# Attention scores by half pieces: column scores and row scores in the two halves of the same PSUM banks

## The chip, the cores and the metric

The kernel runs on one core of one Trainium2 chip. The metric is the device time of one execution in microseconds. The kernel before took 2210.52 us (median of three runs, 2204.25 to 2211.26).

## What is computed

The reference is a two-layer perceiver. 32 batches of 64 latent rows with 256 features go through a first layer (a linear mix with the mean of a context, self-attention, a routed mixture of experts) and a second layer (cross-attention to the context, a convolution with a gated recurrence, a feed-forward block with quantised weights). The part that this change touches is the cross-attention of the second layer, whose context has 1601 rows a batch:

```python
q = _split_heads(query @ Wq.T + bq)      # 16 heads of 16
k = _split_heads(bank @ Wk.T + bk)
v = _split_heads(bank @ Wv.T + bv)
scores = jnp.einsum('bhqd,bhkd->bhqk', q / score_scale, k)
attn = jax.nn.softmax(scores, axis=-1)
ctx = jnp.einsum('bhqk,bhkd->bhqd', attn, v)
return ctx.transpose(0, 2, 1, 3).reshape(b, sq, MODEL_DIM) @ Wo.T + bo
```

All of it is done in float32, but for a bf16 carrier of the maxima that is described below.

## The kernel before, in words

The 2048 latent rows are 16 tiles (`NT`) of 128 rows, each of two batches. For one tile the cross-attention is cut into four halves (two batches by two groups of eight heads), and the context of a half into three pieces of 512 rows (`PIECE`), with a tail of 65 rows (`TAIL`) that all four halves share as one more piece. So a tile has 13 pieces (`NU`), and the program has 208, numbered g.

A piece goes through these steps, each a function of g:

- `keys` (line 671): the projection of 512 context rows to keys, four matmul records of 512 columns on PE (each float32 matmul shows as two records), and one ACT step that adds the bias and leaves `kt` in SBUF (line 692).
- `row_scores` (line 713): the scores with latent rows on the partitions, 128 x 512 for each of four pairs of heads. The four pairs lie on the four row groups of PE's array (32 rows each) and write four banks, which are two tiles `ps[0]` and `ps[1]` of two banks. They serve only for the maximum along the context: two DVE reductions of 1024 elements (line 732; line 729 for the tail).
- `maxima` and `maxima_rows` (lines 734 and 745): when the three pieces of a half and the tail have been scanned, the negated maximum is split into three bf16 parts and transposed to `neg`.
- `column_scores` (line 752): the same scores with context rows on the partitions. A bf16 matmul (line 767, line 764 for the tail) first writes the negated maxima, then 16 float32 matmuls of 128 columns (line 773) add the scores. Again two tiles of two banks; two ACT exponentials of 1024 elements (line 779) write `pt`.
- `values` (line 694): the projection of the piece to values, 16 records on PE, and a DVE copy to one of five buffers `vau` (line 709).
- `weighted` (line 782): 64 records of 64 columns (line 797) add the weighted values of a piece, and a row of ones beside them the denominators, to one accumulator `w.o` in PSUM (pool `ps_o`, one buffer), which is copied to `w.osb` at the tile's end (lines 802 and 804).
- `normalise` (line 806): one quarter of a tile is divided by its sums, with a matmul, a reciprocal (line 815) and a product (line 816).

The score tiles of both kinds come from one pool `ps_sc` with two buffers (line 63), so the four banks are used in turn by columns and rows. Everything else that goes through PSUM shares three banks (`mm_tile`).

The order on PE, DVE, ACT and POOL is that of the program, written out by hand. The loop at line 1256 does for each g: the columns of g, the values of g+4, a share of the other layers' work (`run(g, 0)`), the rows of g+5, the weighted values of g, the keys of g+6, and another share (`run(g, 1)`). The other layers' work (first layer of later tiles, second layer of earlier tiles, routing) consists of generators whose steps `run` deals out by a table of first and last times (lines 1194 to 1209); steps whose result ACT has to take go to place 0 in some of them, the others to place 1. Ahead of the loop the rows of the pieces 0 to 4 are scanned without columns (line 1234). Loads run on SP's queue: `load_batch` (line 1005) brings the context of a batch, 1601 KB, and is called for the next tile at the pieces 2 and 9 of a tile.

Of the kernel before, what the change touches and what calls it, by code (L numbers as in the profile page):

```python
# [9 lines left out]
F32 = mybir.dt.float32  # L10
# [15 lines left out]
NF = 6  # L26
HID = 1024
PIECE = 512
NP = L // PIECE
TAIL = L - NP * PIECE  # L30
NU = 4 * NP + 1
# [13 lines left out]
def perceiver_kernel(ctx: ExitStack, tc: tile.TileContext, a: dict, out: bass.AP):  # L45
# [17 lines left out]
    def sc_tile(name):  # L63
        return ps_sc.tile([P, 2, 512], F32, tag="sc", name=name)
# [571 lines left out]
    def split(g):  # L636

        pos, p = divmod(g, NU)
        if p == 3 * NP:
            return pos, None, None  # L640
        p -= p > 3 * NP
        return pos, 4 * pos + p // NP, p % NP

    def scanned(g):

        pos, p = divmod(g, NU)
        return (pos, 4 * pos + (p - 1) // NP, (p - 1) % NP) if p else (pos, None, None)
# [62 lines left out]
            v[:kr, :, 0:VW - 16].rearrange("p k (h d) -> p k h d", d=17)[:, :, :, 0:16],  # L710
            o[:kr].rearrange("p k (h d) -> p k h d", d=16))

    def row_scores(g):


        pos, h, k = scanned(g)
        w, qbd = wholes[pos], queries[pos]
        if h is None:
            w.mx = small.tile([P, 4, 4, NP + 1], F32, tag="mx1", name=f"mx1_{w.ti}", bufs=2)
        ps = [sc_tile(f"r_{g}_{m}") for m in range(2)]  # L720
        for q in range(4) if h is None else [h % 4]:
            for i in range(4):
                r = slice(32 * i, 32 * i + 32)
                o = ps[i // 2][:, i % 2, :] if h is not None else ps[i // 2][:, i % 2, q * TAIL:(q + 1) * TAIL]
                nc.tensor.matmul(o, lhsT=qbd[r, q % 2, q // 2].rearrange("p h q -> p (h q)"),  # L725
                                 rhs=w.kt[r, q, :] if h is None else halves[h].kt[k][r, :], start=True, stop=True)
        for m in range(2):
            if h is None:
                nc.vector.tensor_reduce(w.mx[:, 2 * m:2 * m + 2, :, NP],
                                        ps[m][:, :, :4 * TAIL].rearrange("p i (q l) -> p i q l", q=4), AX.X, ALU.max)  # L730
            else:
                nc.vector.tensor_reduce(w.mx[:, 2 * m:2 * m + 2, h % 4, k], ps[m], AX.X, ALU.max)  # L732

    def maxima(h):

# [13 lines left out]
        hf.neg = work.tile([P, P], BF16, tag="neg", name=f"neg_{hf.name}", bufs=5)  # L749
        nc.vector.tensor_copy(hf.neg, t)  # L750

    def column_scores(g):

        pos, h, k = split(g)
        w, qbd = wholes[pos], queries[pos]
        ps = [sc_tile(f"s_{g}_{m}") for m in range(2)]
        kr = TAIL if h is None else P
        for i in range(4):
            r = slice(32 * i, 32 * i + 3)
            o = ps[i // 2][:kr, i % 2, :]  # L760
            if h is None:

                for q in range(4):
                    nc.tensor.matmul(o[:, q * P:(q + 1) * P], lhsT=onesb[r, :kr], rhs=halves[4 * pos + q].neg[r, :],
                                     start=(q == 0), stop=False)
            else:
                nc.tensor.matmul(o, lhsT=onesb[r, :], rhs=halves[h].neg[r, :].unsqueeze(1).to_broadcast([3, 4, P]),  # L767
                                 start=True, stop=False)
        for j in range(4):
            q = j if h is None else h % 4  # L770
            for i in range(4):
                r = slice(32 * i, 32 * i + 32)
                nc.tensor.matmul(ps[i // 2][:kr, i % 2, j * P:(j + 1) * P],  # L773
                                 lhsT=w.kt[r, j, :] if h is None else halves[h].kt[k][r, j * P:(j + 1) * P],
                                 rhs=qbd[r, q % 2, q // 2].rearrange("p h q -> p (h q)"), start=False, stop=(j == 3))
        w.pt[g] = []
        for m in range(2):
            pt = big.tile([P, 2, 4, P], F32, tag="pt", name=f"pt_{g}_{m}", bufs=2)
            nc.scalar.activation(pt[:kr].rearrange("p i k c -> p i (k c)"), ps[m][:kr], AF.Exp)  # L779
            w.pt[g].append(pt)  # L780

    def weighted(g):

        pos, h, k = split(g)
        w = wholes[pos]
        first, last = g % NU == 0, g % NU == NU - 1
        if first:
            w.o = o_tile([P, 4, 2, S], f"o1_{w.ti}")
        v, pts = vau[g % 5], w.pt.pop(g)
        kr = TAIL if h is None else P  # L790
        for j in range(4):
            q = j if h is None else h % 4
            for m in range(2):
                for c in range(4):
                    hd = 4 * m + c

                    nc.tensor.matmul(w.o[32 * c:32 * c + 32, q, m, :], lhsT=v[:kr, j, 17 * hd:17 * hd + 32],  # L797
                                     rhs=pts[m][:kr, c // 2, j, c % 2 * S:c % 2 * S + S],
                                     start=(m == 0 and (first and j == 0 or h is None and j == 3)), stop=(m == 1 and (last and j == 3 or h is None and j == 2)))
        if h is None:  # L800
            w.osb = work.tile([P, 4, 2, S], F32, tag="osb", name=f"osb_{w.ti}", bufs=1)
            nc.vector.tensor_copy(w.osb[:, 0:3], w.o[:, 0:3])
        elif last:
            nc.vector.tensor_copy(w.osb[:, 3], w.o[:, 3])
# [407 lines left out]
    with tc.manual_schedule(engines={ET.PE, ET.DVE, ET.Activation, ET.Pool}):  # L1212
        ahead, beside, summing = Steps(first()), Steps(first_layer(1, 1)), Steps(early_sums())
        early = [lambda g=g: keys(g) for g in range(1, 4)] + [lambda: keys(0)] + [
            lambda g=g: values(g) for g in range(4)] + [lambda g=g: keys(g) for g in range(4, 6)]

        def others():
            if 0 in csums:
# [12 lines left out]
                late.pop()()  # L1231
        for f in early + late:
            f()
        for g in range(4):
            row_scores(g)
            others()
        maxima(0)
        row_scores(4)
        others()
        maxima_rows(0)  # L1240
        if beside.gen is not None:
# [14 lines left out]
        for g in range(NU * NT):  # L1256
            pos, p = divmod(g, NU)
            if pos + 1 < NT:
                if p == 0:
                    wholes[pos + 1].rest = load_rest(order[pos + 1])  # L1260
                if p in (2, 9):
                    load_batch(2 * pos + 2 + p // 8)
            column_scores(g)
            if g + 4 < NU * NT:
                values(g + 4)
            if p == 0 and pos:
                normalise(pos - 1, 3)
            elif p > 3 * NP:
                normalise(pos, p - 3 * NP - 1)
            if g + 4 < NU * NT and scanned(g + 4)[2] == NP - 1:  # L1270
                maxima_rows(scanned(g + 4)[1])
            run(g, 0)
            if g + 5 < NU * NT:
                row_scores(g + 5)
                if scanned(g + 5)[2] == NP - 1:
                    maxima(scanned(g + 5)[1])
            weighted(g)
            if g + 6 < NU * NT:
                keys(g + 6)
            if p == 1 and pos:  # L1280
                x4[pos - 1] = projected(pos - 1)
            run(g, 1)
        normalise(NT - 1, 3)
        x4[NT - 1] = projected(NT - 1)
        plan.append(Steps(second_layer(NT - 1)))
# [52 lines left out]
```

## Time and profile before

| | |
|---|---|
| median of three runs | 2210.52 us |
| the profiled execution's own time | 2210.8 us |
| its span | 2209.1 us |
| mean granted PE clock | 0.971 |
| DVE row maxima, 1024 elements (line 732) | 384 times, 1220 ns |
| ACT exponentials, 1024 elements (line 779) | 416 times, 1021 ns |
| PE row scores, records of 512 columns (line 725) | 1536, 228.5 us |
| PE column scores, records of 128 columns (line 773) | 6144, 209.4 us |
| PE bf16 maxima, records of 512 columns (line 767) | 768, 80.6 us |

The span is the time between the first and the last instruction of the profiled execution. In the page's rows, a group of instructions has its line, its engine, what it writes and reads, the busy time in us and the mean of one in ns, and after the second bar the idle time of the engine just before it and what ended it. PE is the matmul engine and PEld its weight loads, DVE the vector engine, ACT the scalar engine. Matmul records are pipelined: a record lasts longer than the distance to the next one, so distances between starts tell what a step costs.

### The profile page before, as it was taken

To read this page: it belongs to the slowest core of one execution; us is meant where nothing else is said; L and a number is where in the kernel's file an instruction comes from. 1 tells how busy PE (TensorE), PEld (TensorE's weight loads), DVE (VectorE), ACT (ScalarE), POOL (GpSimd) and SP (SyncE) were. 2 spreads that over 40 slices of the span, in tenths; PEclk is the share of its full clock that TensorE was granted. 3 is DMA by queue.
4 is the path that set the end of the run, shared out by engine and by line. 5 is a ranking of instruction groups with operands and counts; after the bars stand their busy time and mean duration, and the time that the engine had idled before them with its cause. 6 is when DMAs were issued, how large, how long until landed. Compare 5 with 4: busy or idle time off the path is not lost. (4 is left out here: it accounts for less than half of the span.)

```text
span 2209.1 us, 69768 instructions
## 1 busy us (share of the span) xinstructions
PE 2077.7 (94%) x31887; PEld 1520.5 (69%) x31903; DVE 1342.9 (61%) x2686; ACT 907.4 (41%) x1397; POOL 315.5 (14%) x525
## 2 busy tenths in 40 slices
PE   6799999999999999999999999999998899999984
PEld 4567677677676777777776776777776566677763
DVE  4556765666656566665665656565667656656554
ACT  3334444444435344444544444353433234334342
POOL 2111111111211111111111111111100000000011
PEclk8799999999999999999999999999999999999986
DMA  7223221111212111111211111101100101000000
GB/s 263 87 100 112 80 77 64 64 52 34 70 66 73 64 53 64 37 67 63 76 52 64 66 34 66 64 34 41 37 32 34 42 31 34 14 32 35 2 4 5
DMA packets 46175, 126.41 MB, mean 57 GB/s; under 512 B 12558, under 2 KB 28344, under 8 KB 45880
## 3 DMA queue, kind: packets, MB, share of 16 engines
q1 hardware_dynamic: 45320, 121.13, 16.0%
q8 instruction: 250, 4.10, 0.8%
q10 hardware_dynamic: 560, 0.81, 0.1%
q14 instruction: 45, 0.37, 0.1%
HBM read 119.83 MB, written 2.10 MB: 55 GB/s over the span
## 5 line engine op out<-in xcount | busy, mean ns | idle before, releaser
L779 ACT ACTIVATE pt<-s 128x1024 f32<-128x1024 f32 (+1 forms) x416 | 403.1, 1021 | 307.9 <-PE s L773 307.7
L732 DVE TENSOR_REDUCE mx<-r 128x2 f32<-128x1024 f32 x384 | 452.2, 1220 | 114.3 <-PE r L725 113.9
L233 PE MATMUL vps<-w_L_xattn_WvT,ctxT 128*128 128x128 f32 x3072 | 397.7, 283 | 0.0
L233 PE MATMUL kps<-ctxT,w_L_xattn_WkT 128*128 128x512 f32 x768 | 382.9, 622 | 11.4 <-DMA ctxT<-ctxT 11.4
L692 ACT ACTIVATE kt<-kps,chv 128x512 f32<-128x512 f32 x192 | 131.9, 687 | 636.7 <-PE kps L233 636.7
L709 DVE COPY vau<-vps 128x512 f32<-128x512 f32 (+1 forms) x208 | 143.3, 689 | 399.5 <-PE vps L233 399.5
L233 PEld LDWEIGHTS vps<-w_L_xattn_WvT,ctxT 128*128 128x128 f32 x3072 | 361.6, 193 | 24.1 <-issue 3.4
L797 PEld LDWEIGHTS o<-pt,vau 128*32 128x32 f32 (+1 forms) x13312 | 197.7, 111 | 150.9 <-issue 144.2
L797 PE MATMUL o<-pt,vau 128*32 128x64 f32 (+1 forms) x13312 | 232.3, 222 | 4.2 <-ACT pt L779 4.2
L725 PE MATMUL r<-kt,qbd 32*128 32x512 f32 x1536 | 228.5, 652 | 2.4 <-DVE mx L732 1.5
L233 PEld LDWEIGHTS kps<-ctxT,w_L_xattn_WkT 128*128 128x128 f32 x768 | 131.5, 191 | 123.0 <-issue 106.0
L773 PEld LDWEIGHTS s<-qbd,kt 32*128 32x128 f32 x6144 | 208.6, 189 | 3.2
L773 PE MATMUL s<-qbd,kt 32*128 32x128 f32 x6144 | 209.4, 273 | 0.0
L245 ACT ACTIVATE part<-part 128x1601 f32<-128x1601 f32 x60 | 92.6, 1543 | 16.2 <-DMA part<-ctxT 15.9
L725 PEld LDWEIGHTS r<-kt,qbd 32*128 32x128 f32 x1536 | 63.6, 186 | 40.8 <-issue 19.1
L767 PE MATMUL s<-neg,onesb 3*128 3x512 bf16 x768 | 80.6, 388 | 9.2 <-DVE mx L732 6.9
L767 PEld LDWEIGHTS <-onesb 3*128 3x128 bf16 x768 | 21.3, 91 | 97.6 <-issue 96.2
L815 DVE RECIPROCAL rs<-sums 128x128 f32<-128x128 f32 x64 | 60.7, 948 | 3.4 <-PE sums L812 3.3
L233 PE MATMUL ff<-nT,w_fg 128*128 128x128 f32 x384 | 51.7, 287 | 1.0 <-ACT nT L927 1.0
L311 POOL TENSOR_TENSOR kbd<-kT,mask 128x512 f32<-128x512 f32 x32 | 32.9, 1049 | 138.0 <-ACT kT L304 138.0
L233 PE MATMUL ff<-nT,w_fv 128*128 128x128 f32 x384 | 50.2, 283 | 0.0
L233 PEld LDWEIGHTS ff<-nT,w_fg 128*128 128x128 f32 x384 | 47.8, 201 | 1.9 <-ACT nT L927 1.8
(338 smaller groups left out, 2539.4 us busy)
## 6 DMA issues: line engine op xcount, KB each, us to landing
ctxT<-ctxT SPq DMA_DIRECT2D x32, 1601.0 KB, 6.9
part<-ctxT SPq DMA_DIRECT2D x60, 800.5 KB, 4.5
rest<-ctxT SPq DMA_DIRECT2D x32, 65.0 KB, 2.1
x<-x SPq DMA_DIRECT2D x16, 128.0 KB, 2.6
out<-x SPq DMA_DIRECT2D x16, 128.0 KB, 1.7
w<-w SPq DMA_DIRECT2D x16, 128.0 KB, 2.3
sum_L_ffn_w1T<-L_ffn_w1T SPq DMA_DIRECT2D x4, 256.0 KB, 6.7
raw_L_ffn_w1T<-L_ffn_w1T SPq DMA_DIRECT2D x4, 256.0 KB, 2.6
```

The source lines that it names most:

```text
L233: nc.tensor.matmul(o, lhsT=lhsT(c), rhs=rhs(c), start=(c == 0), stop=(c == 1))
L245: nc.scalar.activation(junk, src, AF.Copy, accum_out=csum[:, c, b:b + 1])
L311: nc.gpsimd.tensor_tensor(kbd[oc], kT[:, oc, :].rearrange("p (b k) -> p b k", b=2).unsqueeze(2).to_broadcast([P, 2, 4, S]), mask4.unsqueez ...
L692: nc.scalar.activation(kt, o, AF.Identity, bias=chv[:, hf.oc, BK2:BK2 + 1])
L709: nc.vector.tensor_copy(v[:kr, :, 0:VW - 16].rearrange("p k (h d) -> p k h d", d=17)[:, :, :, 0:16], o[:kr].rearrange("p k (h d) -> p k h ...
L725: nc.tensor.matmul(o, lhsT=qbd[r, q % 2, q // 2].rearrange("p h q -> p (h q)"), rhs=w.kt[r, q, :] if h is None else halves[h].kt[k][r, :], ...
L732: nc.vector.tensor_reduce(w.mx[:, 2 * m:2 * m + 2, h % 4, k], ps[m], AX.X, ALU.max)
L767: nc.tensor.matmul(o, lhsT=onesb[r, :], rhs=halves[h].neg[r, :].unsqueeze(1).to_broadcast([3, 4, P]), start=True, stop=False)
L773: nc.tensor.matmul(ps[i // 2][:kr, i % 2, j * P:(j + 1) * P], lhsT=w.kt[r, j, :] if h is None else halves[h].kt[k][r, j * P:(j + 1) * P], ...
L779: nc.scalar.activation(pt[:kr].rearrange("p i k c -> p i (k c)"), ps[m][:kr], AF.Exp)
L797: nc.tensor.matmul(w.o[32 * c:32 * c + 32, q, m, :], lhsT=v[:kr, j, 17 * hd:17 * hd + 32], rhs=pts[m][:kr, c // 2, j, c % 2 * S:c % 2 * S ...
L815: nc.vector.reciprocal(rs, t)
```

## The change

The scores are made by halves of a piece, 256 context rows at a time. For half 0 and again for half 1 of each piece, PE writes the column scores of piece g to the first 256 columns of each of the four banks, and right behind them the row scores of piece g+5 to the other 256 columns of the same banks. The exponentials and the maxima of a half then take 512 elements each, in the order exp 0, max 1, exp 1, max 0, so that ACT and DVE work on different tiles. The maxima of a half piece have a place of their own in `mx` (seven instead of four columns). `pt` has six buffers of half the size. The weighted values run half a piece behind: in the iteration of g PE adds the second half of g-1 and the first half of g. The values are made for g+3 instead of g+4, the batches are loaded at the pieces 3 and 10, and the quarters of `normalise` come one piece later, two of the last tile behind the loop.

```diff
+HALF = PIECE // 2
...
+    def row_scores(g, half, ps):
...
-            w.mx = small.tile([P, 4, 4, NP + 1], F32, tag="mx1", name=f"mx1_{w.ti}", bufs=2)
-        ps = [sc_tile(f"r_{g}_{m}") for m in range(2)]
-        for q in range(4) if h is None else [h % 4]:
+        if h is None and half == 0:
+            w.mx = small.tile([P, 4, 4, 2 * NP + 1], F32, tag="mx1", name=f"mx1_{w.ti}", bufs=2)
+        for n, q in enumerate((2 * half, 2 * half + 1) if h is None else [h % 4]):
             for i in range(4):
                 r = slice(32 * i, 32 * i + 32)
...
+                o = ps[i // 2][:, i % 2, HALF:]
...
+                    kt = halves[h].kt[k][r, half * HALF:(half + 1) * HALF]
+                nc.tensor.matmul(o, lhsT=qbd[r, q % 2, q // 2].rearrange("p h q -> p (h q)"), rhs=kt,
+                                 start=True, stop=True)
...
+            nc.vector.tensor_reduce(mx[:, :, h % 4, 2 * k + half], ps[m][:, :, HALF:], AX.X, ALU.max)
...
+    def column_scores(g, half, ps):
...
-                nc.tensor.matmul(o, lhsT=onesb[r, :], rhs=halves[h].neg[r, :].unsqueeze(1).to_broadcast([3, 4, P]),
+                nc.tensor.matmul(o, lhsT=onesb[r, :], rhs=halves[h].neg[r, :].unsqueeze(1).to_broadcast([3, 2, P]),
                                  start=True, stop=False)
-        for j in range(4):
...
+        for j in range(2):
+            n = 2 * half + j
...
+    def exponentials(g, half, ps, m):
+        pos, h, k = split(g)
+        kr = TAIL if h is None else P
+        pt = big.tile([P, 2, 2, P], F32, tag="pt", name=f"pt_{g}_{half}_{m}", bufs=6)
+        nc.scalar.activation(pt[:kr].rearrange("p i k c -> p i (k c)"), ps[m][:kr, :, 0:HALF], AF.Exp)
+        wholes[pos].pt[g, half, m] = pt
+
+    def scores(g, half):
+
+        ps = score_banks(f"s_{g}_{half}")
+        column_scores(g, half, ps)
+        more = g + 5 < NU * NT
+        if more:
+            row_scores(g + 5, half, ps)
+        exponentials(g, half, ps, 0)
+        if more:
+            row_maxima(g + 5, half, ps, 1)
+        exponentials(g, half, ps, 1)
+        if more:
+            row_maxima(g + 5, half, ps, 0)
...
         for g in range(4):
-            row_scores(g)
+            rows_ahead(g)
             others()
...
-                if p in (2, 9):
+                if p in (3, 10):
                     load_batch(2 * pos + 2 + p // 8)
-            column_scores(g)
-            if g + 4 < NU * NT:
-                values(g + 4)
+            scores(g, 0)
+            if g + 3 < NU * NT:
+                values(g + 3)
             if p == 0 and pos:
-                normalise(pos - 1, 3)
-            elif p > 3 * NP:
-                normalise(pos, p - 3 * NP - 1)
+                normalise(pos - 1, 2)
+            elif p > 3 * NP + 1:
+                normalise(pos, p - 3 * NP - 2)
...
             run(g, 0)
-            if g + 5 < NU * NT:
-                row_scores(g + 5)
-                if scanned(g + 5)[2] == NP - 1:
-                    maxima(scanned(g + 5)[1])
-            weighted(g)
+
+            for piece, half in ([(g - 1, 0)] if p == 1 else []) + [(g - 1, 1), (g, 0)]:
+                if piece >= 0 and (p or piece < g):
+                    weighted(piece, half)
+            scores(g, 1)
+            if g + 5 < NU * NT and scanned(g + 5)[2] == NP - 1:
+                maxima(scanned(g + 5)[1])
+            if p == 0 and pos:
+                normalise(pos - 1, 3)
             if g + 6 < NU * NT:
                 keys(g + 6)
             if p == 1 and pos:
                 x4[pos - 1] = projected(pos - 1)
             run(g, 1)
+        weighted(NU * NT - 1, 1)
+        normalise(NT - 1, 2)
         normalise(NT - 1, 3)
```

## The prediction

> **What bounds the kernel now.** I read the engine shares first, then the slices, then the waits of PE, then one piece in the timeline.
>
> ```profile
> PE 2077.7 (94%) x31887; PEld 1520.5 (69%) x31903; DVE 1342.9 (61%) x2686; ACT 907.4 (41%) x1397; POOL 315.5 (14%) x525
> ...
> PE   6799999999999999999999999999998899999984
> PEclk8799999999999999999999999999999999999986
> ```
>
> PE is busy 94% of the span; its gaps lie in the first two and last two slices. In stretches cut by the windows view, PE is idle 8.3 us of 165 to 500 and 8.9 and 9.8 us of the next two 500 us, at full clock. So the piece loop is bound by PE's own stream, and the question is how long that stream becomes and whether new waits tear holes in it. The waits of PE that belong to the scores:
>
> ```profile
> PE s L767 <- DVE mx L732: 6.9, 9, 2.2
> PE r L725 <- ACT pt L779: 6.0, 14, 0.5
> ...
> PE o L797 <- ACT pt L779: 4.2, 8, 0.8
> ...
> PE r L725 <- DVE mx L732: 1.5, 3, 1.1
> ```
>
> (us, times, longest.) They are all small: about 13 us can be won there, since the 4.2 and 1.5 us fall outside the loop proper. One piece, the PE rows of the timeline (start, us):
>
> ```profile
> 1003.76 0.39 PE L767 MATMUL s<-neg,onesb 3*128 3x512 bf16 x4
> ...
> 1003.99 1.06 PE L773 MATMUL s<-qbd,kt 32*128 32x128 f32 x32
> ...
> 1004.98 2.05 PE L233 MATMUL vps<-w_L_xattn_WvT,ctxT 128*128 128x128 f32 x16
> ...
> 1009.75 1.14 PE L725 MATMUL r<-kt,qbd 32*128 32x512 f32 x8
> ...
> 1010.82 1.10 PE L797 MATMUL o<-pt,vau 128*32 128x64 f32 x64
> ...
> 1011.85 1.98 PE L233 MATMUL kps<-ctxT,w_L_xattn_WkT 128*128 128x512 f32 x4
> ...
> 1013.77 0.39 PE L767 MATMUL s<-neg,onesb 3*128 3x512 bf16 x4
> ```
>
> From start to start: columns 1.22 us (1003.76 to 4.98), values 1.89, rows 1.07, weighted 1.03, keys 1.92: 7.13 us. The rest of the piece (4.77 less 1.89 between values and rows here) is the other layers' work. The single records inside these rows show what a block consists of. Four matmuls on four row groups start some 7 ns apart and stream together. Column packs follow each other by 111.6 ns; the bf16 pack of 512 columns takes 230 ns to the next start. The two row packs start at 1009.747 and 1010.281, 534 ns apart, though a 512-column f32 pass streams in 427 ns (the keys' spacing): 107 ns are the first f32 weight load, which nothing hides when PE turns from 128-row to 32-row work. After the last pack of any block some 100 ns pass before the next block starts.
>
> **PE's stream after.** Streamed columns are the same. What changes is the number of blocks and packs. Before: [columns], values, [rows], weighted, keys. After: [columns+rows half 0], values, weighted, [columns+rows half 1], keys. Both have five turns, but the lone f32 entry of the rows is gone: rows follow columns in the same array shape, so their weights can load behind the last column pack, and both half blocks are entered with bf16, which shows no such gap. One half: drain 0.10 + bf16 pack of 256 columns 0.107+0.015 (half of the 512's stream, and the rest of its 230 ns) + 4 column packs 4 x 0.1116 + 2 row packs 2 x (0.213+0.005) = 1.10 us; two are 2.21 us against 1.22+1.07 = 2.29. Saving 0.08 us in each of the 203 iterations that hold both: -16.2 us. The five lone row pieces ahead of the loop and the five lone column pieces at its end pay one more entry, 5 x 0.12 x 2 = +1.2.
>
> Here the Trainium skill speaks against the change: "TensorEngine Tiling (Array Packing)", Performance Considerations, gives each matmul about 60 cycles of overhead. The change adds 12 records a piece (rows 8 to 16, bf16 4 to 8). The bf16 pack streams 512 columns in some 215 ns, so at a column a cycle 60 cycles are an estimated 25 ns: 12 x 25 ns x 203 = +61 us, and the saving would become a loss. The row says otherwise: 32 column records of 128 start within 0.78 us, four by four in 111.6 ns, so one further pack costs about 5 ns beyond its columns. I take the row; the four-abreast reading of the rule (+15 us) is one of my bounds. The same page says that changing the tiling mode drains the engine; the 100 ns and 107 ns are that in this trace, and it is why fewer lone entries pay.
>
> **ACT and DVE.** Exponentials go from 416 of 1024 elements to 832 of 512, maxima likewise.
>
> ```profile
> L779 ACT ACTIVATE pt<-s 128x1024 f32<-128x1024 f32 x384 | 372.2, 1021 | 278.9 <-PE s L773 278.8
> ...
> L237 ACT ACTIVATE th<-su 128x256 f32<-128x256 f32 x16 | 6.1, 383 | 8.1 <-PE su L233 8.1
> ```
>
> ```profile
> L732 DVE TENSOR_REDUCE mx<-r 128x2 f32<-128x1024 f32 x384 | 452.2, 1220 | 114.3 <-PE r L725 113.9
> ...
> L729 DVE TENSOR_REDUCE mx<-r 128x8 f32<-128x520 f32 x32 | 20.9, 695 | 12.7 <-PE r L725 12.7
> ```
>
> ACT: (1021-383)/768 = 0.83 ns an element, so 512 take about 0.60 us (bounds 0.58, the plain 512 copy pT<-tpp, and 0.69, the biased kt<-kps). DVE: about 0.69 us. Added busy time: ACT 384 x (2x0.60-1.02) = +69, DVE 384 x (2x0.69-1.22) = +61 us. At 41% and 61% this hides behind PE, as long as the buffers come back in time.
>
> **The wait that counts.** Both score tiles are used by every half block, so the next half block cannot start before the last exponential and maximum. The order makes the two readers cross over: exp 0 with max 1, then exp 1 with max 0, each tile's second reader waiting for its first (the listing of instructions shows these waits). Why: "PSUM — Partial Sum Buffer", PSUM bank collisions, says two engines must not be in one bank at once. No row of before has two readers in one bank; free of that rule the tiles would be back after 0.1+0.60+0.50 = 1.2 us (ACT's pairs overlap by 0.10). With it: exp 0 starts 0.10 after the block (as now), max 1 at 0.03 and ends at 0.72; exp 1 from 0.78 to 1.38; max 0 from 0.76 to 1.45; PE at about 1.5 us. Hand-over between ACT and DVE is taken at 0.06, between the 0.03 and 0.10 seen from PE.
>
> Two gaps must hold that. Between half 0 and half 1: values and weighted, 2.9 us and more; enough. Between half 1 and the next piece: keys alone where no other layer's work stands there. Measured as now (rows' end to the next block, less 1.03 for weighted) this is 1.85 to 1.89 us in 88 of 202 pieces and above 2.0 nearly everywhere else. Slack 0.35 us. With a turn of 1.5 us the sum of shortfalls is 0.1 us, at 2.0 it is 13.5, at 2.3 it is 41 us.
>
> Late starters: 12 times the exp table is reloaded (L779 ACT_TABLE_LOAD, 1.28 us), only when the block is ready. In the changed order all 12 stand before a half 1; for 7 of the 11 before the end phase the gap is the short one: 7 x (1.28-0.38) = +6.3 us. DVE starts maxima over 0.3 us late in 43 of 208 pieces, 22 of them at short gaps; weighted now stands in front of half 1 and gives it 1.03 us to catch up, so I take +3 us (0.5 to 6). ACT behind weighted half 0: exp 1 at 1.4 us against 1.89+0.43 needed; +1.
>
> Removed: the rows' 6.0 us on ACT (the gap gains weighted's 1.03) and about half of the 6.9 us on mx: -9.5.
>
> **Moved steps.** Values one piece later: the stream keeps its 16 records and the DVE copy; one set leaves PE's unbroken stretch before the loop (-1.8) and arrives where PE waits at the end. Maxima ahead of the loop: 1.3 us of DVE and PE at half clock, taking turns twice a piece, +0.6 x 5 = +3. Both batch loads a piece later on SP's queue: 1601 KB land in 6.9 us, the first keys need them five pieces, some 50 us, later: nothing. Normalise 2 moves behind the loop for the last tile: reciprocal 0.95 + multiply 0.31 = +1.3; elsewhere it hides under PE. The last pieces, bound by exp, have shorter steps: -1.
>
> **Sum.** -16.2+1.2 -9.5 +6.3+3+1 -1.8+3+1.3-1 = -12.7 us. The profiled execution took 2210.8 us, 1.7 above its span and at the median of the runs (2210.52). Forecast 2198 us, -0.6%.
>
> **Rivals.** (a) Slower: the crossed turn is longer than keys. If exp is 0.69 us, each hand-over 0.2 and some queue delay is common, the turn is 2.3: +41 us at the short gaps, +28 net, 2239. It turns from gain to loss at about 2.0 us, where the shortfall eats the 12.7. For it: DVE is 61% busy and its delays now also hold exp 1. Against: the known durations give 1.5. 0.20. (b) The rows do not ride free: weights of the first column or row pack are not hidden by a 107 ns pass, 0.04 us per half, +16: 2214, near 2210. For it: half the cover. Against: column packs hide their own loads in 107 ns already. 0.20. (c) The waits were the smaller part and the gain is full: no late-starter cost and columns shorter, 2186. 0.15. The forecast has 0.45, of which 0.03 falls within 0.3%.
>
> Measurement can tell about 0.3% from no change, 2204 to 2217. Range 2180 to 2228: it takes in (c), (b), the four-abreast rule (2213) and the milder half of (a). Faster 0.57, within 0.3% 0.22, slower 0.21.
>
> **What would show it.** Right: in a regular piece two half blocks of 1.10 us start to start; row packs 0.218 apart with no 0.107 at their head; PE's wait for exp or mx below 15 us in all; exp near 0.60, maxima near 0.69. Wrong: PE waiting for ACT or DVE before most half 0 blocks; a half block of 1.2 us; PE's matmul records further apart; PE's idle time in the middle slices above 2%.

## The result and the profile after

The changed kernel takes 2283.62 us (median of four runs, 2278.48 to 2289.98) against 2210.59 for the kernel before beside it: 1.0343 of its time [1.0323, 1.0364], 73 us slower. The forecast was 2198 us with a range of 2180 to 2228. The profiled execution took 2289.98 us with a span of 2288.2 (before 2210.8 and 2209.1), and the mean granted PE clock fell from 0.971 to 0.961.

From the page after, the engine shares, PE's slices and the groups of the changed steps:

```profile
PE 2105.3 (92%) x34191; PEld 1568.8 (69%) x34207; DVE 1394.8 (61%) x3102; ACT 991.7 (43%) x1813; POOL 314.2 (14%) x525
...
PE   6799999999999999999999999989998998899984
PEclk8799999999999999999999999999999898999996
...
L793 ACT ACTIVATE pt<-s 128x512 f32<-128x512 f32 (+1 forms) x832 | 491.7, 597 | 817.9 <-PE s L734 637.5
L744 DVE TENSOR_REDUCE mx<-s 128x2 f32<-128x512 f32 x752 | 494.7, 689 | 410.0 <-PE s L734 385.8
...
L734 PEld LDWEIGHTS s<-kt,qbd 32*128 32x128 f32 x3008 | 120.3, 190 | 24.1 <-ACT kt L693 23.9
```

Exponentials of 597 ns and maxima of 689 ns are what was forecast (0.60 and 0.69 us). PE's busy share fell from 94 to 92%, and more of the slices show eights. PE's busy time rose by 28 us although its stream became shorter: records last longer at half clock, and the modelled ends of matmuls cover some gaps, as shown below.

PE's waits (us, times, longest) now have the changed steps at the head. Before, the longest of these steps were 6.9 us for `mx` and 6.0 for `pt`:

```profile
PE o L826 <- DVE osb L832: 18.4, 14, 2.4
PE o L826 <- ACT pt L793: 15.9, 15, 4.7
PE s L778 <- ACT pt L793: 15.1, 17, 2.7
...
PE tpp L374 <- DVE vau L710: 6.8, 6, 1.6
```

The first two belong to `weighted` (line 826 now), which had 4.2 us of waits before, all for `pt`. The last row shown stands for several: an unrelated step that takes the next of the three shared banks waits until DVE has copied the values out of it. Over all rows for `vau` this is 15.1 us before and 23.4 after.

In a regular half block all went as computed. The timeline of after, second half of one piece and its turn (start, duration, us):

```profile
1007.46 0.60 ACT L793 ACTIVATE pt<-s 128x512 f32<-128x512 f32 x1 [2.27 <-DVE mx L744]
...
1008.11 0.54 PE L826 MATMUL o<-pt,vau 128*32 128x64 f32 x24 [0.38 <-ACT pt L793]
...
1008.59 0.29 PE L778 MATMUL s<-neg,onesb 3*128 3x256 bf16 x4
...
1008.71 0.62 PE L785 MATMUL s<-qbd,kt 32*128 32x128 f32 x16
...
1009.15 0.60 PE L734 MATMUL s<-kt,qbd 32*128 32x256 f32 x8
...
1009.69 1.98 PE L234 MATMUL kps<-ctxT,w_L_xattn_WkT 128*128 128x512 f32 x4
1009.86 0.60 ACT L793 ACTIVATE pt<-s 128x512 f32<-128x512 f32 x1 [1.80 <-PE s L734]
1009.86 1.32 DVE L744 TENSOR_REDUCE mx<-s 128x2 f32<-128x512 f32 x2
...
1010.65 0.60 ACT L793 ACTIVATE pt<-s 128x512 f32<-128x512 f32 x1 [0.19 <-DVE mx L744]
```

The half block is 1.10 us from start to start (1008.59 to 1009.69). Exp 1 waits 0.19 us for max 1, DVE's two maxima take 1.32 us together, and both readers are done by 1011.25, some 1.5 us after the block. The keys of a full piece cover that. (The first two lines belong to half 0 of the same piece: there exp 1 had waited 2.27 us for a maximum, and `weighted` waited for that exponential. This lateness of DVE comes up again below.) What went wrong lies outside the half block, and four places show it.

**Rows right behind the keys they need.** The timeline of after at the start of a piece:

```profile
335.30 0.29 PE L778 MATMUL s<-neg,onesb 3*128 3x256 bf16 x4
...
335.41 0.69 ACT L693 ACTIVATE kt<-kps,chv 128x512 f32<-128x512 f32 x1 [0.47 <-PE kps L234]
...
336.14 0.31 PEld L734 LDWEIGHTS s<-kt,qbd 32*128 32x128 f32 x8 [0.30 <-ACT kt L693]
```

The keys of g+6 end the iteration of g, and the rows of half 0 in the next iteration read exactly those keys. Only the columns with their bf16 pack, 0.56 us in the regular piece above, lie between. ACT's bias step ends at 336.10, so here the rows start 0.84 us after the block's start. The page has this 79 times, 23.9 us, and only in the row of the weight loads: the modelled ends of the column matmuls cover the gap, so PE's own row shows no wait.

**The accumulator behind the tail.** The tail is the tenth piece of a tile and completes three of its four quarters; line 832 copies them (384 columns) out of the accumulator. The timeline of after at this place:

```profile
321.15 0.54 DVE L832 COPY osb<-o 128x384 f32<-128x384 f32 x1
...
321.84 0.65 PE L826 MATMUL o<-pt,vau 128*32 128x64 f32 x32 [1.71 <-ACT s L361]
```

The second half of the tail (it ends at 320.1) and the first half of the next piece now stand side by side on PE and write the same bank, which has to be copied to `osb` in between. The copy starts at 321.15, after other DVE work, and PE starts 0.15 us after its end. (The releaser named, ACT's step of line 361, ends within 0.02 us of the copy, but line 826 reads nothing of it; the copy is what it depends on.) Before, other work of PE lay in this place.

**ACT's own queue at a short gap.** Of the 15.1 us before half blocks, 12.5 stand at one point of eleven tiles, where the keys of the tail and one step of another layer (`pw`, 1.03 us) are all that lies between half 1 and the next piece. The timeline of after at this point:

```profile
426.31 1.16 PE L234 MATMUL kps<-rest,w_L_xattn_WkT 128*128 128x130 f32 x8
426.47 1.28 ACT L793 ACT_TABLE_LOAD   x1 [0.97 <-PE s L734]
...
427.76 1.08 ACT L793 ACTIVATE pt<-s 128x512 f32<-128x512 f32 x2
...
428.90 0.53 PE L778 MATMUL s<-neg,onesb 3*128 3x256 bf16 x4 [0.56 <-ACT pt L793]
```

The exponentials stand behind a reload of ACT's table in all eleven. Six of the waits are 0.56 us, as here; the other five are 0.9 to 2.7 us, with more work late in ACT's queue or DVE's.

**What a wait costs beyond itself.** The windows view of after around this wait (stretch, length, then busy us of PE, PEld, DVE, ACT and POOL with their records, and last the granted clock, DMA share and GB/s):

```profile
320.10:321.80 1.70, 0.03 (x4) 0.00 (x0) 1.30 (x3) 1.70 (x5) 0.62 (x1) 1.00 0.00 0
...
322.70:326.10 3.40, 3.40 (x30) 1.78 (x23) 1.65 (x3) 1.73 (x4) 0.00 (x0) 0.50 0.52 161
```

After 1.7 us without work PE ran 3.4 us at half clock, which loses another 1.7 us; from 326.10 the clock is 1.00 again. Cut finely in the same way, the traces give the whole: in the loop, up to the end phase, the sum of (1 - clock) x time is 12 us in before and 43 us in after, in steps of 1.71. That is 31 of the 79 us between the spans. Over the whole span it is 26, as the end phase loses 5 us less than before. The four runs of the changed kernel bear it out: from the one with the shortest span (2276.7 us at a mean clock of 0.967) to the one with the longest (2288.2 at 0.961), (1 - clock) x span rises from 75 to 89 us. The profiled execution is the longest of the four, so the others lost less of this.

Not every such wait costs it. All changes of the clock in this trace lie on one grid of 3.41 us, and the idle time of PE within one window of the grid tells most of it. In after's loop, none of the 552 windows at full clock with less than 1.4 us of idle time was followed by half clock, 12 of the 21 with 1.4 to 2.0 us were, and all 7 with more. The Trainium skill ("TensorE: Matmul & The Clock Gate", What's actually happening) gives windows of 3.4 us and half rate after one idle window. The length agrees with the 3.4 us here, the threshold doesn't: some half of such a window was enough.

### The profile page after: what moved, and what is told of

Its sections match the earlier page's. It is cut to its first block, busy times and chain, and to the rows that moved or that the text cites. A ratio compares the mean times of both kernels' runs of the same rounds, so it can differ in the third digit from the quotient of the medians.

```text
span 2288.2 us, 75511 instructions
## 1 busy us (share of the span) xinstructions
PE 2105.3 (92%) x34191; PEld 1568.8 (69%) x34207; DVE 1394.8 (61%) x3102; ACT 991.7 (43%) x1813; POOL 314.2 (14%) x525
## 4 chain that ended last, share of the span: by engine, by line
PE 75%; DVE 15%; ACT 6%; issue 2%; DMA 1%; POOL 0%; POOLq 0%; SPq 0%; ACTq 0%; DVEq 0%
PE vps L234 14%; PE kps L234 14%; PE o L826 8%; PE s L734 8%; PE s L785 6%; PE ff L234 4%; DVE mx L744 3%; PE s L778 3%; ACT kt L693 2%; PE ffo L970 2%; DVE vau L710 1%; ACT pt L793 1%; PE wo L862 1%; PE q L234 1%; PE hg L921 1%
## 5 line engine op out<-in xcount | busy, mean ns | idle before, releaser
L793 ACT ACTIVATE pt<-s 128x512 f32<-128x512 f32 (+1 forms) x832 | 491.7, 597 | 817.9 <-PE s L734 637.5
L744 DVE TENSOR_REDUCE mx<-s 128x2 f32<-128x512 f32 x752 | 494.7, 689 | 410.0 <-PE s L734 385.8
L234 PE MATMUL kps<-ctxT,w_L_xattn_WkT 128*128 128x512 f32 x768 | 390.4, 632 | 11.2 <-DMA ctxT<-ctxT 11.2
L826 PE MATMUL o<-pt,vau 128*32 128x64 f32 (+1 forms) x13312 | 243.2, 224 | 38.0 <-DVE osb L832 18.4
L826 PEld LDWEIGHTS o<-pt,vau 128*32 128x32 f32 (+1 forms) x13312 | 204.1, 112 | 78.2 <-issue 39.9
L734 PE MATMUL s<-kt,qbd 32*128 32x256 f32 x3008 | 242.9, 396 | 8.4
L785 PE MATMUL s<-qbd,kt 32*128 32x128 f32 x6144 | 246.2, 277 | 0.0
L734 PEld LDWEIGHTS s<-kt,qbd 32*128 32x128 f32 x3008 | 120.3, 190 | 24.1 <-ACT kt L693 23.9
L778 PE MATMUL s<-neg,onesb 3*128 3x256 bf16 x1536 | 115.6, 282 | 16.0 <-ACT pt L793 15.1
L778 PEld LDWEIGHTS <-onesb 3*128 3x128 bf16 x1536 | 41.5, 91 | 122.8 <-issue 103.3
```

The source lines that it names most:

```text
L234: nc.tensor.matmul(o, lhsT=lhsT(c), rhs=rhs(c), start=(c == 0), stop=(c == 1))
L744: nc.vector.tensor_reduce(mx[:, :, h % 4, 2 * k + half], ps[m][:, :, HALF:], AX.X, ALU.max)
```

## The experiments

Three theories stood at the start: the waits of `weighted` and of the rows for `kt` (places in the order), the crossed turn of ACT and DVE (the prediction's rival a), and the reload of ACT's table. All ratios are to the kernel before, run on the same chip.

**Where the keys and the weighted values stand.** The first, e1, exchanges the places of keys and values:

```diff
             scores(g, 0)
-            if g + 3 < NU * NT:
-                values(g + 3)
+            if g + 6 < NU * NT:
+                keys(g + 6)
...
-            if g + 6 < NU * NT:
-                keys(g + 6)
+            if g + 3 < NU * NT:
+                values(g + 3)
```

> The changed kernel with keys and values in exchanged places: keys(g+6) between the two half blocks, values(g+3) behind the second. Theory of new waits: in the changed kernel the rows of half 0 stand right behind the keys and wait some 0.30 us for the ACT step that writes kt, in about 80 pieces (weight loads of the rows idle 23.9 us for kt); with the keys earlier that is gone: about 24 us less, 2260, and the distance from the columns' start to the rows' start is 0.45 us in every half block. Rival, the halving itself costs PE (more records, more packs): within 5 us of 2284. Rival, the two readers of one bank are the cost: within 5 us of 2284, since both gaps keep their length.

Measured 2341.01 us, 1.0612 [1.0589, 1.0636]: missed by 81 us. The rows' wait for `kt` is gone from the page, and six of the 13 pieces of a tile are 0.2 to 0.4 us shorter than in after (medians). But ACT's bias step now stands between the half blocks, behind exp 1, and three pieces are 0.9 to 1.8 us longer. The timeline of e1, ACT alone, and one of PE's waits:

```profile
341.11 0.60 ACT L793 ACTIVATE pt<-s 128x512 f32<-128x512 f32 x1 [2.40 <-DVE mx L744]
341.60 0.68 ACT L693 ACTIVATE kt<-kps,chv 128x512 f32<-128x512 f32 x1
```

```profile
PE tpp L374 <- ACT kt L693: 10.4, 5, 2.7
```

Exp 1 waited 2.40 us for a maximum that DVE had not reached, the bias step behind it kept its shared bank for as long, and another layer's transposes (line 374) waited for the bank. So a wait of ACT for DVE is passed on to whoever waits for ACT's next step. Over all rows PE now waits 38.7 us for `kt`, where after has none of it outside the weight loads, and 54.1 us for exponentials, where after has 31.9.

In e2 the weighted values come a whole piece late, so that the exponentials have that much longer and other work stands between tail and next piece again:

```diff
-            for piece, half in ([(g - 1, 0)] if p == 1 else []) + [(g - 1, 1), (g, 0)]:
-                if piece >= 0 and (p or piece < g):
-                    weighted(piece, half)
+            for half in range(2):
+                if g:
+                    weighted(g - 1, half)
...
+        weighted(NU * NT - 1, 0)
         weighted(NU * NT - 1, 1)
```

> The changed kernel with the weighted values a whole piece behind (both halves of g-1 in the iteration of g) instead of half a piece. Theory of new waits: PE's 38 us of idle time ahead of weighted go (18 us for the copy of the accumulator at a tile's tenth piece, 20 us for exponentials that DVE or ACT made late); about 30 us less, 2254, as some of the lateness comes out at the next block. Rival, halving itself costs PE: within 5 us of 2284. Rival, two readers in one bank: the copy's 18 us go, the rest comes back at the next half block, 2266.

Measured 2241.18 us, 1.0151 [1.0131, 1.017]: 42 us less than after, more than expected. The waits of line 826 are gone from the list. In the loop the clock's loss falls from 43 to 27 us, so about 15 of the 42 are clock. What is left has 19.5 us of waits for `pt` before half blocks, and in the waits of the weight loads of e2 the rows still stand as in after:

```profile
PEld s L734 <- ACT kt L693: 23.0, 77, 0.3
```

Then both edits together (e3), and e3 with an exponential of one column behind the last gelu, so that ACT's table is back before it is needed (e4):

```diff
+    tiny = const.tile([P, 1], F32, name="tiny")
...
             nc.scalar.activation(h[:, 512 * j:512 * j + 512], h_ps, AF.Gelu, scale=d)
+        nc.scalar.activation(tiny, mhalf, AF.Exp)
```

> Both edits together: keys between the half blocks, and weighted a whole piece behind. Theory of new waits: the two gains add up to 50 to 60 us, about 2229; what is left over before is ACT's table loads and DVE's late starts. Rival, halving itself costs PE: above 2270. Rival, two readers in one bank: about 2250.

> As the run before it, and behind the two gelu steps of a tile ACT computes one exponential of a single column, so that its table is loaded back while it has nothing else to do and not when a score block is ready (one small ACT step a tile more). Theory of new waits: PE's 15 us of waiting for exponentials ahead of half 0 shrink to some 4: about 11 us less than the run before it, 2218. Rivals: no change, ACT is busy 43% only.

Measured 2288.52 us, 1.0374 [1.0349, 1.0399], and 2298.95 us, 1.0407 [1.0387, 1.0427]. Both missed: e3 for e1's reason (PE waits 36.8 us for `pt` before a half block, 33 times, and 38.9 for `kt` over all rows), and the earlier table takes nothing off (37.5 us, 33 times). In e3's trace the gelu steps, the reload and the exponentials already follow each other in ACT's queue at the point shown above; e4 only moves the reload within this row of steps, and the waits there grow by about 0.1 us each. So e4 does not show that the reload costs nothing. It cannot be the main cause for another reason: the waits of after that stand behind it are the 12.5 us above. Of the 10 us of e4 over e3, 6 are clock (from 94 to 100 us of (1 - clock) x time in the profiled executions); the rest stays open.

The wait for `kt` can also be removed by earlier keys instead of another place. In e5, on top of e2, the keys are one more piece ahead in the same place:

```diff
-        kt = big.tile([P, PIECE], F32, tag="kt", name=f"kt_{hf.name}_{k}", bufs=7)
+        kt = big.tile([P, PIECE], F32, tag="kt", name=f"kt_{hf.name}_{k}", bufs=8)
...
-            if g + 6 < NU * NT:
-                keys(g + 6)
+            if g + 7 < NU * NT:
+                keys(g + 7)
```

> The changed kernel with weighted a whole piece behind (as e2_piece_behind) and the keys one piece further ahead: keys(g+7) in the place of keys(g+6), with eight buffers kt (to make room for it: four buffers neg in place of five, two ng in place of three). Nothing moves past another engine's work but the keys themselves. Theory of new waits: the rows' wait for kt (23 us in e2_piece_behind) goes and no new wait comes, since the kt step stays behind the same exponentials: 2241 - 23 = 2218. The loss of the exchange in e1_keys_first was then due to kt between the two half blocks, where ACT has its side work. Rival, the kt wait only hid another one (the turn of the tiles): within 6 us of 2241.

Measured 2219.33 us (2218.04 to 2219.56), 1.0051 [1.0036, 1.0066]: as expected, 22 us below e2 for a wait of 23.0 us that is no longer in the list. Of the 73 us, 64 are now taken away by two edits of the order. But the new order was to be faster, and it still is 11 us slower.

**What is left: DVE's queue.** In e5 the waits for `vau` are 27.2 us over all rows. The timeline of e5 at the last piece of a tile (place 12; places count from 0, so that the tail is place 9):

```profile
460.56 1.22 DVE L939 TENSOR_TENSOR_SCAN rr<-zz,gg 96x512 f32<-96x512 f32 x1
...
462.23 1.25 DVE L744 TENSOR_REDUCE mx<-s 128x2 f32<-128x512 f32 x2
...
462.98 0.60 ACT L793 ACTIVATE pt<-s 128x512 f32<-128x512 f32 x1 [2.39 <-DVE mx L744]
...
463.40 0.68 DVE L710 COPY vau<-vps 128x512 f32<-128x512 f32 x1
...
464.14 0.65 PE L374 MATMUL tpp<-ident,s 128*128 128x128 f32 x4 [1.99 <-DVE vau L710]
```

The scores were complete at 459.9. From 459.25 on DVE is in a chain of another layer's work (lines 934 to 939 and a normalisation) that stands ahead of the two maxima in its queue, and reaches them at 462.23. Exp 1 waits for the first of them; the copy of the values, which stands behind both, ends at 464.08; PE, which needs its bank, stands still for 1.99 us. Before, this queue had one pair of maxima a piece; now two pairs have to get past the same side work.

To weigh this by itself, e7 and e9 shorten the maxima, e7 those of e5:

```diff
-            nc.vector.tensor_reduce(mx[:, :, h % 4, 2 * k + half], ps[m][:, :, HALF:], AX.X, ALU.max)
+            nc.vector.tensor_reduce(mx[:, :, h % 4, 2 * k + half], ps[m][:, :, HALF:HALF + 32], AX.X, ALU.max)
```

and e9 those of the kernel before:

```diff
-                nc.vector.tensor_reduce(w.mx[:, 2 * m:2 * m + 2, h % 4, k], ps[m], AX.X, ALU.max)
+                nc.vector.tensor_reduce(w.mx[:, 2 * m:2 * m + 2, h % 4, k], ps[m][:, :, 0:64], AX.X, ALU.max)
```

e6 exchanges the places of e5's side work:

```diff
-                if (self.kind == ACT) != (place == 0):
+                if (self.kind == ACT) != (place == 1):
...
-                planned(sums(pos, 3), max(t0 - 14, 7), t0 - 1, 17, 0)
+                planned(sums(pos, 3), max(t0 - 14, 7), t0 - 1, 17, 1)
```

and e8 halves the operations of the kernel before and nothing else, the maxima in the same way as the exponentials:

```diff
-            nc.scalar.activation(pt[:kr].rearrange("p i k c -> p i (k c)"), ps[m][:kr], AF.Exp)
+            for half in range(2):
+                nc.scalar.activation(pt[:kr, :, 2 * half:2 * half + 2].rearrange("p i k c -> p i (k c)"),
+                                     ps[m][:kr, :, 256 * half:256 * half + 256], AF.Exp)
```

> As e5_keys_lead7, and the other layers' steps change places: those that need ACT run behind the second half block, the others between the two, and the context sums too run behind the second half block. Theory of deadlines: ACT's side work (table loads, gelu, sums of 1.5 us) then stands ahead of half 0, whose tiles are needed only after values and weighted (2.9 us), not ahead of half 1, whose tiles are needed after the keys (1.85 us): PE's 19 us of waiting for exponentials go down to below 10, time 10 us less than e5_keys_lead7, about 2208. Rival: DVE's side work is the one that is late, and it now stands ahead of half 1: more waits on mx, 5 to 15 us slower than e5_keys_lead7.

> As e5_keys_lead7, but the row maxima of the full pieces look at 32 of the 256 columns only (224 columns are left out of the maximum), so that a maximum takes about 0.2 us instead of 0.69 and the turn of a tile pair about 1.3 us instead of 1.5. Theory that ACT and DVE are coupled by the crossed order: what DVE is late goes, 10 to 20 us less than e5_keys_lead7, about 2203. Rival, DVE is not what is left: within 5 us.

> The kernel before, with each exponential and each row maximum of a full piece in two instructions of 512 elements, and nothing else: 832 exponentials, 752 maxima, as in the changed kernel (and mx with seven columns), PE as before. If half-size steps of ACT and DVE as such cost time: above 2230. Theory of new waits: they hide behind PE in the old order, 0 to 12 us slower than before.

> The kernel before, with row maxima of the full pieces over 64 of 512 columns (448 columns are left out of the maximum): the control of e7_short_maxima. Theory that the changed order made DVE's time count: before, it hid, so that only PE's 7 us of waiting for maxima and the few us of DVE ahead of the loop go: 2195 to 2203. Rival, DVE's 300 us cost PE time in any order (a shared port, waits of the other layers): about 2165, as in e7_short_maxima.

Measured: e6 2299.18 us, 1.0414 [1.0397, 1.0432]; e7 2165.95, 0.9811 [0.9797, 0.9826]; e8 2216.21, 1.0042 [1.0027, 1.0057]; e9 2184.37, 0.989 [0.9876, 0.9905].

e6 went the rival's way and much further, 80 us above e5. Of PE's waits in e6 this one stands first:

```profile
PE s L778 <- ACT pt L793: 60.1, 45, 3.8
```

Most of the waits before half blocks now stand behind the keys or behind the side work that follows them. So the side work's place is not free to choose either. e8 hit: halving the operations costs 8 us in the old order.

e7 and e9 are the pair that settles most, though both lie outside what was expected of them: e7 gained 53 us on e5 and not 10 to 20, and e9 fell between its theory and its rival. The engine shares on the pages of e7 and e9:

```profile
PE 2043.9 (94%) x34191; PEld 1540.6 (71%) x34207; DVE 1058.0 (49%) x3102; ACT 959.4 (44%) x1813; POOL 314.3 (15%) x525
```

```profile
PE 2061.6 (94%) x31887; PEld 1510.3 (69%) x31903; DVE 991.5 (45%) x2686; ACT 907.7 (42%) x1397; POOL 314.1 (14%) x525
```

One of PE's waits, first in e5 and then in e7:

```profile
PE s L778 <- ACT pt L793: 22.0, 30, 2.4
```

```profile
PE s L778 <- ACT pt L793: 3.0, 9, 0.7
```

With DVE at 49% the half blocks wait 3.0 us for `pt`, where e5 had 22.0, and PE is 94% busy again. e7 against e9 compares the two orders with DVE out of the way: 0.9811/0.989 = 0.992, about 18 us less (each interval is some 3 us wide to a side). PE's busy time falls by 17.7 us between the two. The forecast had -16.2+1.2 = -15 us for PE's stream; neither of the two numbers is the stream alone, since waits and clock differ as well, but a saving of the forecast's size is there.

The long maxima cost 53 us in the new order (e5 to e7) and 24 in the old (before to e9): 29 us more, for nearly the same DVE time (334 and 351 us). The traces name the parts. From e5 to e7 PE's waits for `pt` fall by 19 us, those for `vau` by 15, and the clock's loss by 20. From before to e9 the waits for `mx` fall by 6, those for `vau` by 2, and the clock's loss by 14. And -18+29 = +11 is what e5 has, by the way the four kernels are compared. How much of the 29 is the lateness and how much the halving itself, which costs 8 us in e8, no run separates.

**Can the queue be relieved?** Four kernels on top of e5. In e10 the copy of the values goes to ACT:

```diff
-        nc.vector.tensor_copy(
+        nc.scalar.copy(
```

in e12 only at three places of a tile:

```diff
-        nc.vector.tensor_copy(
+        (nc.scalar.copy if (g - 3) % NU in (0, 8, 12) else nc.vector.tensor_copy)(
```

In e11 the values come behind the side work:

```diff
             scores(g, 0)
-            if g + 3 < NU * NT:
-                values(g + 3)
...
             run(g, 0)
+            if g + 3 < NU * NT:
+                values(g + 3)
```

and in e13, at place 12 alone, they are issued ahead of the exponentials and maxima of half 0:

```diff
             row_scores(g + 5, half, ps)
+        if half == 0 and g % NU == 12 and g + 3 < NU * NT:
+            values(g + 3)
         exponentials(g, half, ps, 0)
...
-            if g + 3 < NU * NT:
+            if p != 12 and g + 3 < NU * NT:
                 values(g + 3)
```

> As e5_keys_lead7, but ACT instead of DVE copies the values to vau (143 us of DVE's busy time go, ACT has some 0.6 us a piece more). Theory that DVE's queue is what is late: the values' banks come back without the side work and the two maxima ahead of them, PE's 25 us of waiting for vau go, half of it comes back as waits on ACT: about 2207. Rival, ACT's queue is as late, being tied to DVE by the crossed order: 2219 or more.

> As e5_keys_lead7, but the other layers' steps between the half blocks stand ahead of the values instead of behind them. Theory that the vau copy, which waits in DVE's queue behind side work and maxima, keeps a bank from the other layers' steps: these no longer wait for it, 8 to 12 us less, 2209. Rival: the side work itself waits for DVE, nothing changes, within 4 us of 2219.

> As e5_keys_lead7, with ACT copying the values only in the iterations 0, 8 and 12 of a tile, where the pieces are longer than before by 0.1, 0.7 and 1.3 us. Theory that DVE is late there: two thirds of these 2.1 us a tile go, some 20 us less in all, 2200 and below the kernel before. Rival, ACT is late at the same places: no gain.

> As e5_keys_lead7, and at the last piece of each tile the values and their copy to vau are issued ahead of the exponentials and maxima of half 0, so that DVE's queue has side work, vau, maxima there instead of side work, maxima, vau. Theory that the maxima ahead of vau cost 1.25 us a tile at that piece: 15 x 1.2 = 18 us less than e5_keys_lead7, 2201, 0.3% faster than the kernel before; PE's 22 us of waiting for vau go to about 5. Rival, DVE is late by its side work alone and what is taken there comes out as a wait for the maxima at half 1: within 5 us of 2219.

Measured: e10 2220.69 us, 1.0057 [1.0039, 1.0075]; e11 2314.07, 1.0477 [1.0459, 1.0495]; e12 2217.51, 1.0037 [1.0022, 1.0051]; e13 2207.93 (22 runs), 0.9987 [0.9978, 0.9996].

e10 changed nothing, and the timeline of e10, ACT alone, says why:

```profile
463.40 0.60 ACT L793 ACTIVATE pt<-s 128x512 f32<-128x512 f32 x1 [2.40 <-DVE mx L744]
463.89 0.58 ACT L710 COPY vau<-vps 128x512 f32<-128x512 f32 x1
```

The copy stands behind exp 1, exp 1 behind max 1, max 1 behind DVE's side work: by the crossed order the two queues act as one. Here the rival hit, and so it did in e12, which gained 2 us, within its uncertainty. e11 missed both of its forecasts and lost 95 us. PE now waits 19.9 and 17.7 us for POOL's quantisation steps (9.0 and 9.7 in e5), and the clock loses 29 us more; that the side work follows itself too closely without the values between is my reading, and half of the 95 us is not accounted for. The first of the two in e11's waits:

```profile
PE tpq_h L997 <- POOL q_h L992: 19.9, 14, 4.9
```

e13 is the one that helped: 11 us below e5, where 18 were expected. In the timeline of e13, the same place:

```profile
459.31 0.66 DVE L710 COPY vau<-vps 128x512 f32<-128x512 f32 x1
459.89 1.28 DVE L744 TENSOR_REDUCE mx<-s 128x2 f32<-128x512 f32 x2
...
460.02 0.66 PE L374 MATMUL tpp<-ident,s 128*128 128x128 f32 x4 [0.79 <-DVE vau L710]
```

The copy is ahead of the maxima and PE waits 0.79 us instead of 1.99; the waits for `vau` fall to 14.7 us in all, before's level. The time is with that of the kernel before, 0.13% below it, too little to be told from no change by the 0.3% of the prediction. What is left in e13 before half blocks is 24.3 us of waits for `pt` and 9.0 for the maxima of the tail. They are of three kinds, and the timeline of e13 shows the first two, at place 6 and behind it:

```profile
536.82 1.28 DVE L744 TENSOR_REDUCE mx<-s 128x2 f32<-128x512 f32 x2
537.60 0.60 ACT L793 ACTIVATE pt<-s 128x512 f32<-128x512 f32 x1 [3.02 <-DVE mx L744]
...
538.25 0.29 PE L778 MATMUL s<-neg,onesb 3*128 3x256 bf16 x4 [1.34 <-ACT pt L793]
...
539.36 1.16 PE L234 MATMUL kps<-rest,w_L_xattn_WkT 128*128 128x130 f32 x8
...
540.95 0.29 PE L778 MATMUL s<-neg,onesb 3*128 3x256 bf16 x4 [0.43 <-ACT pt L793]
```

Some 17 us stand between half 0 and half 1 (mostly at places 6 and 8), where DVE chains of 3 to 5 us are ahead of the maxima of half 0. Some 6 us stand behind the keys of the tail, which take 1.16 us and not 1.98: e5's earlier keys have moved them to a gap without side work, and there the turn of 1.5 us is too long. Another 6 us stand behind ACT's own chain of gelu and table reload. In e7, where only the maxima are shorter, the three come down to 7.5, 0.4 and 3.2 us; moving these steps by themselves was not tried.

## Why the prediction was wrong

**Right.** The sizes: half block 1.10 us, exponentials 597 ns, maxima 689, a turn of 1.5 us, and for PE's stream -15, where the two orders differ by -18 with short maxima. The decision for the row against the Trainium skill's 60 cycles a matmul ("TensorEngine Tiling (Array Packing)", Performance Considerations) held: 12 more records a piece, and the half block is as long as the sum without them. Rival (b), weights of rows not riding free, is out in pieces where `kt` is there: rows start 0.44 us behind the columns, four packs of 0.11 us. Whether the 107 ns that went were the first weight load or a drain between modes (the prediction names both), no run separates.

**Wrong, the step that failed.** It is the part on the waits, which looked at one wait only: "The wait that counts", the two score tiles. For every other operand of the moved steps it took the cover from the old order.

- "rows follow columns in the same array shape, so their weights can load behind the last column pack": true of the array, but who makes these weights was not asked. In the old order columns, values and side work stood between keys and rows; in the new one 0.56 us of columns do. 22 us (e2 to e5).
- "Between half 0 and half 1: values and weighted, 2.9 us and more; enough." `weighted` was counted as cover and not as a waiter. It waits for exp 1 of the block just before it, priced +1 and measured 15.9, and behind the tail for the copy of its accumulator, which the sum does not have: 18.4. With the clock, 42 us (e2). Exp 1 was itself late where a maximum was late (the 2.27 us shown above), so this term and the next share a cause: e2 took away the waiter, e7 the lateness.
- "I take +3 us (0.5 to 6)" for DVE's late maxima. Measured as the difference of two pairs, 29 us. It looked only at starts late for the short gap before the next piece; most of the costs lay at the first half, where exp 1, then the copy of the values, then a shared bank and another layer's step wait in line behind the same DVE chain.
- The granted clock was priced for the stretch ahead of the loop only. In the loop, waits that add up to about half of a 3.41-us window mostly cost 1.7 us more; 31 us of the span's 79 (contained in the sizes above).

The account by the runs: -18 (the new order with short maxima) +22 (`kt`) +42 (`weighted`) +29 (the long maxima) = +75 us, measured +73. That it closes is no further proof, since the runs form a chain from before over e5 and e2 to after; what they show is the size of each step.

Rival (a) had the sign and one clause of the cause ("its delays now also hold exp 1"), but not the mechanism: the turn was 1.5 us and not 2.3. The late table load was in the right place and half of its size: +6.3 in the sum, 12.5 measured at that gap, since the reload was priced alone and other work in the queues was late with it in five of eleven tiles. One reading of the lines was incomplete: before's slices show two eights in the later part of the loop as well, not only at the ends (28.7 us of idle time between 1500 and 2000 us, 40.4 in after). The signs set beforehand did speak: PE idle in the middle slices above 2% (between 500 and 1500 us it is 4.6%, 46.0 us of 1000), and waits for `pt` and `mx` above 15 us.

## What to carry to other kernels

When a step moves in an order written by hand, list for each of its operands and for its accumulator who makes it or frees it, on which queue, and how much work now lies between; a saving in one engine's stream says nothing on that. Splitting a stage in two doubles its deadlines while the side work ahead of it in the same queues keeps its length. Two readers crossed over two tiles tie their two queues together, so that moving work from one to the other gained nothing here (e10). To separate the saving from the lateness, shorten the suspected engine's work in both orders and compare the pair.

## What the hardware showed that was not expected

- A wait of PE of 1.7 us, no more, was followed by 3.4 us at a granted clock of 0.50; the loss came in steps of 1.71 us, 7 of them in before's loop and 25 in after's. In after's loop the idle time within one window of a grid of 3.41 us went with it: below 1.4 us no window was followed by half clock, above 2.0 us every one, and between them about half.
- A gap in front of a matmul in the middle of a block appears only in the row of the weight loads: 23.9 us in after that PE's waits do not list. e5 shows that they were real, 22 us of time.
- Two maxima back to back took 1.32 us together, where twice 689 ns would be 1.38: by their records they overlap a little.
